# Softplus from the scalar engine's logarithm, the second expert share added there, and cluster prompts summed by steps

## The chip, the cores and the metric

The kernel runs on one core of a Trainium2 chip. A core has five engines, each with its own instruction queue, worked off in order: PE (TensorE, matrix products and transposes into PSUM), DVE (VectorE, element by element), ACT (ScalarE, functions from activation tables, copies, scaling), POOL (GpSimd, which here issues gathers and scatter-adds by row number) and SP (which issues plain DMAs). An engine waits for another only where a semaphore says so. The metric is the device time of one execution in microseconds, the median over several runs.

## The reference

The input `x` is (2, 2048, 256): two batches of 2048 tokens with 256 channels, all in 32-bit floats. Each token is normalised, and three things are added: `x` itself, a state-space scan over the tokens sorted by cluster, and a mixture of experts.

```python
xn = layernorm(x)
# scan branch, per batch
bucket = argmax(l2norm(xn) @ l2norm(means).T)         # 8 clusters
xs     = xn sorted by bucket (stable)
dts, Bm, Cm = split(x_proj @ xs)                      # 32, 16 and 16 rows
Cm    += (means @ prompt_weight.T)[bucket]            # the cluster's prompt
delta  = softplus(dt_proj @ dts + dt_bias)            # 256 channels
h_t    = exp(delta_t * A) * h_(t-1) + delta_t * u_t * B_t   # 16 states a channel
y_t    = sum over states of h_t * C_t + Ds * u_t      # then put back in token order
# expert branch
p1, p2 = softmax of the two largest of xn @ w_gate    # 8 experts
ffn    = sum over the two experts of p * ((silu(xn @ w1) * (xn @ w3)) @ w2)
out    = x + scan + ffn
```

Softplus is log(1 + exp(v)). The kernel writes it as max(v, 0) + log(1 + e) with e = exp(-|v|).

## The kernel before, in words

The front (about the first 65 us) loads `x`, normalises it, finds clusters and experts, and writes the normalised rows with four more columns to the DRAM tensor `xn`. Columns D to D+3 of a row hold the first expert, the second share, the first share minus the second, and the second expert.

From then on two streams of work run interleaved.

*The scan.* The sorted tokens are cut in 8 pieces of 512 (class `Piece`; two batches by four). The 256 channels are two halves `h` of 128 partitions. A piece is prepared by `gather` (four indirect DMAs into `xs`), `turn` (transposes into `u`), `find_members` (which of the 8 clusters each position belongs to, the tile `member`), `project` and `end_projection` (the product `px`, in which `member` by the small matrix `cp` adds the prompts), `load_b` and `load_z` (DMAs that spread rows of B and C) and `step_size`, `square` and `series`, which make `dl` (delta) and `du` (delta by u). Then come 8 steps for each piece (class `Step`: four groups of 4 states by two halves). A step has four places `i`. At each, `feed` makes `bu` on DVE, `scan` runs one recurrence over 512 tokens on DVE, and `decay` makes the `da` of the next step on ACT by an exponential. One step later, `turn` transposes the states on PE into a pair of PSUM buffers (`pt_s`), ACT copies them out (`ht`), and `contract` multiplies them by C on PE into `y`.

*The experts.* The token-expert pairs are sorted into 71 tiles of 128 rows (class `Tile`). A tile has its row gather `load_rows` (tile `xg_sb`, four buffers), `turn` (transposes `pt_g`, the copy `xT`, and the row's share `own`), two `up` products (`p_ps`, with a tanh `t_sb` on ACT, and `silu` and `gate` on DVE), and `down` (product `py`, scaled by `own` on ACT into `yo`, and added to DRAM rows by an indirect DMA on POOL). Weights come by the indirect DMAs `load_up` and `load_down`, three buffers each. A tile that has the same expert as the one three before it is given row numbers out of bounds, so its fetch moves nothing.

*The order.* Every engine's order is the order in which the text emits instructions; a chain of dependencies at the end of the kernel pins it. A planner writes that text. The work on pieces is put at places by `at_place(step, place, ...)`, with place divided by 4 carried into the step. Tile work is a list of `jobs` (two `up` parts and one `down` part for each tile), given out at the places so that the summed PE cost keeps a fixed ratio to the summed DVE cost; the costs are the last two arguments of `at_place`. `silu` and `gate` come two places after their `up`. In the `down` part of tile t the text emits `turn` of tile t+2, the row gather of tile t+5, then the products, `yo` and the scatter-add of tile t, and then the `w_down` fetch of tile t+3; the second `up` part of tile t emits the `w_up` fetch of tile t+3. All these DMAs share POOL's one queue. The first piece is prepared before any step runs, in the list `lead`, one entry after each of the first 13 jobs.

Lines that the prediction's steps touch: the polynomial (L702 `square`, L713 and L718 and L722 `series`), `step_size` (L692 to L698), `own` (L862, L866), `yo` (L902), row gather (L849), weight fetches (L835), scatter-add (L816), gather of a piece (L620), the copies `ht` (L791) and `xT` (L860), the exponential `da` (L760), the scan (L775), the product for the prompts `pc` (L283).

Of the kernel before, what the change touches and what calls it, by code (L numbers as in the profile page):

```python
# [40 lines left out]
F32 = mybir.dt.float32  # L41
BF16 = mybir.dt.bfloat16
I32 = mybir.dt.int32
AF = mybir.ActivationFunctionType
ALU = mybir.AluOpType
# [4 lines left out]
P = 128  # L50
CH = 512
LN_EPS = 1e-5
NORM_EPS_SQ = 1e-24
LOWEST = -3.0e38

LOG1P = (
    (1.0093577, 1.1060627), (-0.08225194, 3.2574694), (-1.424736, 2.702104), (-2.321687, 0.43240654),
)
LOG1P_C = 0.0052326876


@with_exitstack
def scan_moe_kernel(
# [14 lines left out]
    nc = tc.nc  # L78
# [39 lines left out]
    line_of = [cst.tile([P, J], I32, name=f"line_of{b}") for b in range(B)]  # L118
    token_of = cst.tile([P, NT], I32, name="token_of")
    first = [cst.tile([K, NCH], F32, name=f"first{b}") for b in range(B)]  # L120
    last = [cst.tile([K, NCH], F32, name=f"last{b}") for b in range(B)]
    ROWS = B * L + TS
    xn_d = dram.tile([ROWS, D + SH], F32, name="xn")
    acc_d = dram.tile([ROWS, D], F32, name="acc")
# [74 lines left out]
        spare, pattern=[[0, 1]], base=B * L + 1, channel_multiplier=1,  # L199
        allow_small_or_imprecise_dtypes=True,  # L200
    )
    log1p_a = cst.tile([P, len(LOG1P)], F32, name="log1p_a")
    for i, (a, _) in enumerate(LOG1P):
        nc.vector.memset(log1p_a[:, i : i + 1], a)
    zero = cst.tile([P, D + SH], F32, name="zero")
    nc.vector.memset(zero, 0.0)
    te8 = cst.tile([P, NT], F32, name="te8")
# [65 lines left out]
    def small_weights():  # L273

        diag = cst.tile([P, ND, P], F32, name="diag")
        for h in range(ND):
            nc.vector.tensor_scalar(diag[:, h, :], ident, dcol[:, h : h + 1], None, ALU.mult)

        cp = cst.tile([K, XP], F32, name="cp")
        nc.vector.memset(cp, 0.0)  # L280
        pc = ps_m.tile([K, NS], F32, tag="m", name="pc")
        for h in range(ND):
            nc.tensor.matmul(  # L283
                pc, lhsT=chosen_by[:, h, 0:K], rhs=pwT[:, h, :], start=h == 0, stop=h == ND - 1
            )
        nc.vector.tensor_copy(cp[:, R + NS :], pc)

        nc.scalar.activation(na, na, AF.Exp)
        nc.vector.tensor_scalar_mul(na, na, -1.0)
        return diag, cp  # L290
# [146 lines left out]
    def sort_tokens():  # L437
# [55 lines left out]
        nc.vector.tensor_copy(pos, posf)  # L493
        for b in range(B):
            nc.vector.tensor_scalar(first[b], begins, fst[:, b : b + 1], None, ALU.add)
            nc.vector.tensor_scalar(last[b], first[b], cntT[:, b : b + 1], None, ALU.add)
        return pos

    def list_rows(b: int, pos):
# [126 lines left out]
    class Piece:  # L626
# [17 lines left out]
        def find_members(self):  # L644
            b, c = self.b, self.c
            self.member = scn.tile([K, CH], F32, tag="member", name="member", bufs=1)
            nc.vector.tensor_scalar(self.member, at, first[b][:, c : c + 1], None, ALU.is_ge)
            nc.vector.scalar_tensor_tensor(
                self.member, at, last[b][:, c : c + 1], self.member, ALU.is_lt, ALU.mult
            )  # L650

        def project(self, h: int):
            if h == 0:
# [31 lines left out]
        def step_size(self, h: int):  # L685

            if h == 0:
                self.e = pre.tile([P, ND, CH], F32, tag="tok", name="e")
                self.r = pre.tile([P, ND, CH], F32, tag="tok", name="r")
                self.sq = {}  # L690
            pd = ps_m.tile([P, CH], F32, tag="m", name="pd")
            nc.tensor.matmul(  # L692
                pd, lhsT=dtT[:, h * P : (h + 1) * P], rhs=self.xd[0:R, :], start=True, stop=True
            )
            nc.scalar.activation(self.e[:, h, :], pd, AF.Abs, bias=bias[:, h : h + 1])
            nc.scalar.activation(self.r[:, h, :], pd, AF.Relu, bias=bias[:, h : h + 1])  # L696

            nc.scalar.activation(self.e[:, h, :], self.e[:, h, :], AF.Exp, scale=-1.0)  # L698

        def square(self, h: int, i: int):  # L700
            self.sq[h, i] = scn.tile([P, CH], F32, tag="sq", name="sq", bufs=3)
            nc.scalar.activation(  # L702
                self.sq[h, i], self.e[:, h, :], AF.Square, bias=log1p_a[:, i : i + 1]
            )

        def series(self, h: int, i: int):

            if h == 0 and i == 0:
                self.dl = prep.tile([P, ND, CH], F32, tag="dl", name="dl")
                self.du = prep.tile([P, ND, CH], F32, tag="du", name="du")  # L710
            dl = self.dl[:, h, :]
            if i < len(LOG1P):
                nc.vector.scalar_tensor_tensor(  # L713
                    dl, self.sq.pop((h, i)), LOG1P[i][1], dl if i else self.e[:, h, :],
                    ALU.add, ALU.mult,
                )
            elif i == len(LOG1P):
                nc.vector.scalar_tensor_tensor(  # L718
                    dl, dl, LOG1P_C, self.r[:, h, :], ALU.mult, ALU.add
                )  # L720
            else:
                nc.vector.tensor_mul(self.du[:, h, :], dl, self.u[:, h, :])  # L722

        def begin(self, h: int):

# [104 lines left out]
    class Tile:  # L830
# [23 lines left out]
        def turn(self):  # L854
            xg = self.xg
            pt = ps_m.tile([P, ND, P], F32, tag="m", name="pt_g")
            for h in range(ND):
                nc.tensor.transpose(pt[:, h, :], xg[:, h * P : (h + 1) * P], ident)  # L858
            self.xT = ffn.tile([P, ND, TS], F32, tag="xT", name="xT")
            nc.scalar.copy(self.xT, pt)  # L860
            self.own = ffn.tile([P, 1], F32, tag="own", name="own", bufs=6)
            nc.vector.scalar_tensor_tensor(  # L862
                self.own, xg[:, D : D + 1], te8[:, self.t : self.t + 1], xg[:, D + 2 : D + 3],
                ALU.is_equal, ALU.mult,
            )
            nc.vector.tensor_add(self.own, self.own, xg[:, D + 1 : D + 2])  # L866

        def up(self, i: int):
            wk = w13_sb[self.t % NW][:, i * ND * H : (i + 1) * ND * H].rearrange(
# [24 lines left out]
        def down(self):  # L894
            w2 = w2_sb[self.t % NW].rearrange("p (f d) -> p f d", f=NH)
            py = ps_m.tile([P, D], F32, tag="m", name="py")
            for f in range(NH):
                nc.tensor.matmul(  # L898
                    py, lhsT=self.g[:, f, :], rhs=w2[:, f, :], start=f == 0, stop=f == NH - 1
                )  # L900
            yo = ffn.tile([P, D], F32, tag="yo", name="yo", bufs=3)
            nc.scalar.activation(yo, py, AF.Copy, scale=self.own)  # L902
            add_rows(acc_d, [(token_of[:, self.t : self.t + 1], yo)])

# [85 lines left out]
    turn_tile(1)  # L990
    p = pieces[0]

    def first_series(h: int):
        for i in range(len(LOG1P) + 2):
            if i < len(LOG1P):
                p.square(h, i)
            p.series(h, i)


    lead = [  # L1000
        [lambda: list_rows(0, pos)], [p.gather], [], [], [], [lambda: p.turn(0)],
        [lambda: p.turn(1), p.find_members],
        [lambda: p.project(0), lambda: p.project(1), p.end_projection],
        [lambda: p.load_b(0), *(lambda q=q: p.load_z(q) for q in range(NQ)), lambda: p.step_size(0)],
        [lambda: p.step_size(1), lambda: first_series(0)], [lambda: first_series(1)],
        [lambda: p.begin(0), lambda: p.begin(1)], [lambda: p.mask_z(0)],
    ]
    ahead = len(lead)
# [26 lines left out]
    for n, p in enumerate(pieces):  # L1035
        s0 = n * SP_
        for q in range(1, NQ):
            at_place(max(s0 + 2 * q - 3, 0), NSUB - 1 if n or q > 1 else 0, lambda p=p, q=q: p.load_b(q))
        if n:
            s1 = s0 - SP_  # L1040
            at_place(max(s1 - 1, 0), 1 if n > 1 else 0, p.gather)
            for h in range(ND):
                at_place(s1 + 1, 2 + h, lambda p=p, h=h: p.turn(h), 0.5)
                at_place(s1 + 2, 1 + 2 * h, lambda p=p, h=h: p.project(h), 0.95)
                at_place(s1 + 3 + h, 2 - 2 * h, lambda p=p, h=h: p.step_size(h), 1.0)
                for i, place in enumerate(((17, 18, 20, 21, 23, 25), (19, 22, 24, 26, 28, 30))[h]):
                    if i < len(LOG1P):
                        at_place(s1, place - 2, lambda p=p, h=h, i=i: p.square(h, i))
                    at_place(s1, place, lambda p=p, h=h, i=i: p.series(h, i), 0.0, 0.6)
            at_place(s1 + 2, 0, p.find_members, 0.0, 1.2)  # L1050
            at_place(s1 + 3, 0, p.end_projection, 0.95)
            for q, load, use in ((0, 16, 22), (1, 20, 27), (2, 29, 33), (3, 37, 41)):
                at_place(s1, load, lambda p=p, q=q: p.load_z(q))
                at_place(s1, use, lambda p=p, q=q: p.mask_z(q), 0.0, 0.6)
            at_place(s1 + 5, NSUB - 1, lambda p=p: p.load_b(0))
            at_place(s0, 3, lambda p=p: p.begin(0), 0.9)
            at_place(s0 + 1, 1, lambda p=p: p.begin(1), 0.9)
        s2 = s0 + SP_
        to = acc_d if n + 1 < len(pieces) else out_rows
        at_place(s2, 0, lambda p=p: p.take_sums(0))  # L1060
        at_place(s2, 3, lambda p=p: p.take_sums(1))
        at_place(s2 + (n + 1 < len(pieces)), 0 if n + 1 < len(pieces) else 3, lambda p=p, to=to: p.add_sums(to))
# [106 lines left out]
```

## Time and profile before

| what | value |
|---|---|
| three runs | 793.4, 794.46, 795.9 us (median 794.46) |
| profiled execution, its own time | 793.45 us |
| its span, first to last instruction | 791.7 us, 16967 instructions |
| mean granted TensorE clock | 0.951 |
| last expert product `py` starts | 749.1 us |
| last `yt` copy of the scan starts | 779.5 us |
| DMA | 125.90 MB, mean 159 GB/s |

The span is cut in 40 slices of 19.8 us. The first four are the front; the preparation of the first piece lies between 69 and 117 us; the two streams run interleaved from there to about 749 us; after that only the last four scan steps and the output are left. Busy shares are averages over these stages, so a stage is read by its own window. An engine's "idle before" is attributed to the event that released it.

### The profile page before, as it was taken

The numbers are of one execution on the slowest core, as the hardware profiler recorded it, in microseconds if no ns is written. First come the engines' busy times: TensorE is split into PE (matmuls) and PEld (weight loads), VectorE is DVE, ScalarE is ACT, GpSimd is POOL, SyncE is SP. The second block draws the span as 40 slices with busy tenths as digits, with TensorE's granted clock in tenths as the row PEclk, the third lists the DMA queues.
The fourth block names the chain that finished last, engine by engine and source line by source line (L and its number), as shares of the span: only waits on it lengthen the run. The fifth ranks groups of instructions, "written<-read, shape, count | busy, mean of one in ns | idle before, by whom it ended". The sixth has DMA issues, their size and how long they took to land.

```text
span 791.7 us, 16967 instructions
## 1 busy us (share of the span) xinstructions
PE 712.9 (90%) x6552; PEld 605.5 (76%) x6552; DVE 711.3 (90%) x1162; ACT 507.9 (64%) x986; POOL 520.9 (66%) x374
## 2 busy tenths in 40 slices
PE   7385979899999999899999999999999998999963
PEld 5144768589877988599868986798779885998842
DVE  8865269899999999899989999899999998899991
ACT  4821266586669657776668666866687576757572
POOL 2023738657867886788776787878678787686313
PEclk9755999999999999999999999999999998999996
DMA  8593244664368547855656367448644855444462
GB/s 280 222 323 114 58 173 108 210 172 97 108 155 244 154 106 215 203 148 143 206 140 176 56 247 219 107 95 263 197 111 132 273 156 112 107 102 96 86 219 27
DMA packets 61215, 125.90 MB, mean 159 GB/s; under 512 B 24464, under 2 KB 42032, under 8 KB 53776
## 3 DMA queue, kind: packets, MB, share of 16 engines
q0 software_dynamic: 40224, 65.03, 34.6%
q1 hardware_dynamic: 20912, 59.80, 22.1%
q8 instruction: 52, 0.85, 0.4%
q14 instruction: 27, 0.22, 0.1%
HBM read 180.06 MB, written 27.00 MB: 262 GB/s over the span
## 4 chain that ended last, share of the span: by engine, by line
PE 69%; ACT 6%; DVE 3%; issue 3%; DMA 2%; POOL 1%; POOLq 0%; SPq 0%; ACTq 0%; DVEq 0%
PE p_ps L875 28%; PE py L898 14%; PE pt_s L787 12%; PE y L796 6%; ACT ht L791 2%; DMA out_dram<-acc 2%; PE y L728 2%; PE pt_g L858 2%; PE px L655 2%; PE pd L692 1%; DVE hs L775 1%; ACT da L760 1%; DVE bu L766 1%; PE px L660 1%; PE pt_u L641 1%
## 5 line engine op out<-in xcount | busy, mean ns | idle before, releaser
L875 PE MATMUL p_ps<-xT,w 128*128 128x128 f32 x2272 | 280.3, 279 | 5.3 <-ACT sq L702 4.3
L875 PEld LDWEIGHTS p_ps<-xT,w 128*128 128x128 f32 x2272 | 268.2, 195 | 20.2 <-issue 9.3
L775 DVE TENSOR_TENSOR_SCAN hs<-da,carry,bu 128x512 f32<-128x512 f32 x192 | 246.2, 1283 | 0.0
L760 ACT ACTIVATE da<-dl,na 128x512 f32<-128x512 f32 x256 | 182.0, 723 | 1.1 <-DVE hs L775 1.0
L816 POOL DMA_INDIRECT acc<-yo,token_of x71 | 137.8, 1941 | 60.3 <-ACT yo L902 20.0
L766 DVE TENSOR_TENSOR bu<-du,bt 128x512 f32<-128x512 f32 x256 | 174.0, 680 | 0.0
L791 ACT COPY ht<-pt_s 128x512 f32<-128x512 f32 x256 | 137.1, 590 | 31.3 <-PE pt_s L787 31.0
L787 PE MATMUL pt_s<-ident,hs 128*128 128x128 f32 x1024 | 137.9, 279 | 14.7 <-ACT ht L791 8.7
L835 POOL DMA_INDIRECT w<-in_w_up_dram,w_row x71 | 94.8, 1335 | 84.2 <-DVE w_row L584 36.8
L898 PE MATMUL py<-w,g 128*128 128x256 f32 x568 | 139.0, 389 | 12.2 <-ACT r L696 8.7
L787 PEld LDWEIGHTS pt_s<-ident,hs 128*128 128x128 f32 x1024 | 117.7, 143 | 31.6 <-ACT ht L791 15.6
L898 PEld LDWEIGHTS py<-w,g 128*128 128x128 f32 x568 | 104.2, 193 | 27.1 <-ACT r L696 10.3
L849 POOL DMA_INDIRECT xg_sb<-xn,token_of x71 | 88.3, 1243 | 37.5 <-issue 30.2
L835 POOL DMA_INDIRECT w<-in_w_down_dram,w_row x71 | 93.5, 1317 | 21.6 <-issue 12.5
L883 ACT ACTIVATE t_sb<-p_ps 128x512 f32<-128x512 f32 x71 | 42.5, 599 | 69.4 <-PE p_ps L875 69.1
L902 ACT ACTIVATE yo<-py,own 128x256 f32<-128x256 f32 x71 | 33.8, 476 | 80.5 <-PE py L898 80.3
L775 DVE TENSOR_TENSOR_SCAN hs<-da,bu 128x512 f32<-128x512 f32 x64 | 78.2, 1223 | 0.0
L796 PE MATMUL y<-ht,z 128*32 128x128 f32 x2048 | 74.3, 279 | 2.5 <-ACT ht L791 1.9
L816 POOL DMA_INDIRECT acc<-yt,line_of x28 | 54.7, 1952 | 25.7 <-ACT ht L791 8.2
L796 PEld LDWEIGHTS y<-ht,z 128*32 128x32 f32 x2048 | 51.1, 110 | 24.5 <-issue 13.2
L888 DVE SCALAR_TENSOR_TENSOR t_sb<-t_sb,p_ps 128x512 f32<-128x512 f32 x71 | 48.2, 679 | 9.1 <-ACT t_sb L883 8.8
L892 DVE SCALAR_TENSOR_TENSOR g<-t_sb,p_ps 128x512 f32<-128x512 f32 x71 | 48.3, 681 | 7.2 <-PE p_ps L875 4.7
(188 smaller groups left out, 632.8 us busy)
## 6 DMA issues: line engine op xcount, KB each, us to landing
bt<-bc SPq DMA_DIRECT2D x32, 1024.0 KB, 5.4
z<-bc SPq DMA_DIRECT2D x32, 256.0 KB, 3.8
xn<-xt SPq DMA_DIRECT2D x8, 520.0 KB, 2.6
xt<-in_x_dram SPq DMA_DIRECT2D x8, 512.0 KB, 7.5
acc<-in_x_dram SPq DMA_DIRECT2D x8, 512.0 KB, 6.4
w<-in_w_up_dram,w_row POOLq DMA_INDIRECT x71
w<-in_w_down_dram,w_row POOLq DMA_INDIRECT x71
xg_sb<-xn,token_of POOLq DMA_INDIRECT x71
```

Of the source, the lines that this page charges most:

```text
L760: nc.scalar.activation(self.da[i], self.piece.dl[:, self.h, :], AF.Exp, scale=na[:, self.h, n : n + 1])
L766: nc.vector.tensor_mul(self.bu[i], self.piece.du[:, self.h, :], self.piece.bts[self.q][:, i, :])
L775: nc.vector.tensor_tensor_scan(self.hs[:, :, i], self.da[i], self.bu[i], start, ALU.mult, ALU.add)
L787: nc.tensor.transpose(pt[:, j, :], self.hs[:, t0 : t0 + G, :].rearrange("p t n -> p (t n)"), ident)
L791: nc.scalar.copy(self.ht[i], pt)
L796: nc.tensor.matmul(p.ys[self.h][j * G : (j + 1) * G, i, :], lhsT=p.zs[q][:, i * (P // G) + j, :], rhs=self.ht[i][:, j, :], start=False, st ...
L816: ins = nc.gpsimd.indirect_dma_start(out=to, out_offset=bass.IndirectOffsetOnAxis(ap=numbers, axis=0), in_=rows, in_offset=None, compute_o ...
L835: nc.gpsimd.indirect_dma_start(out=to[self.t % NW], out_offset=None, in_=rows, in_offset=bass.IndirectOffsetOnAxis(ap=w_row[:, self.t : se ...
L849: nc.gpsimd.indirect_dma_start(out=self.xg, out_offset=None, in_=xn_d, in_offset=bass.IndirectOffsetOnAxis(ap=token_of[:, self.t : self.t ...
L875: nc.tensor.matmul(p[:, f, :], lhsT=wk[:, h, f * P : (f + 1) * P], rhs=self.xT[:, h, :], start=h == 0, stop=h == ND - 1,)
L892: nc.vector.scalar_tensor_tensor(self.g, self.s, 0.5, self.p3, ALU.mult, ALU.mult)
L898: nc.tensor.matmul(py, lhsT=self.g[:, f, :], rhs=w2[:, f, :], start=f == 0, stop=f == NH - 1)
```

## The change

Three edits are made together.

1. *Softplus.* The polynomial for log(1 + e), e times four quadratics, is replaced; it took four squares on ACT and five multiply-adds on DVE for each half. ACT makes `w` = 1 + e (rounded) and takes its logarithm, one instruction over both halves (128x1024). DVE makes (w - 1) - e, which is what the rounding added, takes it from `r` = max(v, 0), adds `r` to the logarithm and multiplies by `u`, each over both halves at once. The exponential moves out of `step_size` into `decay_of_one`. The planner's places and costs change accordingly.
2. *Share.* `own` is column D+2 where the tile's expert is the row's first one, and zero elsewhere; this is still made on DVE in `Tile.turn`. The addition of the second share moves from there to ACT in `Tile.down`, as the bias of an Identity activation on a 128x1 column, read from `xg`.
3. *Prompts.* `member` is now 1 for every cluster that begins at or before the position, so one comparison makes it. `cp` holds differences between successive clusters' prompts (made from `differ`), so the product sums the steps. The tiles `last` are gone.

```diff
+        differ = cst.tile([P, ND, K], F32, name="differ")
+        nc.vector.tensor_copy(differ[:, :, 0:1], chosen_by[:, :, 0:1])
+        nc.vector.tensor_sub(differ[:, :, 1:], chosen_by[:, :, 1:K], chosen_by[:, :, 0 : K - 1])
...
-                pc, lhsT=chosen_by[:, h, 0:K], rhs=pwT[:, h, :], start=h == 0, stop=h == ND - 1
+                pc, lhsT=differ[:, h, :], rhs=pwT[:, h, :], start=h == 0, stop=h == ND - 1
...
-            nc.vector.tensor_scalar(last[b], first[b], cntT[:, b : b + 1], None, ALU.add)
...
-            nc.vector.scalar_tensor_tensor(
-                self.member, at, last[b][:, c : c + 1], self.member, ALU.is_lt, ALU.mult
-            )
...
+        def decay_of_one(self, h: int):
+            if h == 0:
+                self.w = scn.tile([P, ND, CH], F32, tag="w", name="w", bufs=1)
             nc.scalar.activation(self.e[:, h, :], self.e[:, h, :], AF.Exp, scale=-1.0)
-        def square(self, h: int, i: int):
-            self.sq[h, i] = scn.tile([P, CH], F32, tag="sq", name="sq", bufs=3)
-            nc.scalar.activation(
-                self.sq[h, i], self.e[:, h, :], AF.Square, bias=log1p_a[:, i : i + 1]
-            )
+            nc.scalar.activation(self.w[:, h, :], self.e[:, h, :], AF.Identity, bias=ones[:, 0:1])
+
+        def log(self):
+            self.dl = prep.tile([P, ND, CH], F32, tag="dl", name="dl")
+            nc.scalar.activation(self.dl, self.w, AF.Ln)
+
+        def series(self, i: int):
+            if i == 0:
+                nc.vector.scalar_tensor_tensor(
+                    self.e, self.w, 1.0, self.e, ALU.subtract, ALU.subtract
+                )
+            elif i == 1:
+                nc.vector.tensor_sub(self.r, self.r, self.e)
+            elif i == 2:
+                nc.vector.tensor_add(self.dl, self.dl, self.r)
+            else:
+                self.du = prep.tile([P, ND, CH], F32, tag="du", name="du")
+                nc.vector.tensor_mul(self.du, self.dl, self.u)
...
-            nc.vector.tensor_add(self.own, self.own, xg[:, D + 1 : D + 2])
...
+            nc.scalar.activation(self.own, self.own, AF.Identity, bias=self.xg[:, D + 1 : D + 2])
             nc.scalar.activation(yo, py, AF.Copy, scale=self.own)
...
-        [lambda: p.step_size(1), lambda: first_series(0)], [lambda: first_series(1)],
+        [lambda: p.decay_of_one(0), lambda: p.step_size(1), lambda: p.decay_of_one(1), p.log, lambda: p.series(0),
+         lambda: p.series(1)],
+        [lambda: p.series(2), lambda: p.series(3)],
...
-                for i, place in enumerate(((17, 18, 20, 21, 23, 25), (19, 22, 24, 26, 28, 30))[h]):
-                    if i < len(LOG1P):
-                        at_place(s1, place - 2, lambda p=p, h=h, i=i: p.square(h, i))
-                    at_place(s1, place, lambda p=p, h=h, i=i: p.series(h, i), 0.0, 0.6)
-            at_place(s1 + 2, 0, p.find_members, 0.0, 1.2)
+                at_place(s1, 16 + 2 * h, lambda p=p, h=h: p.decay_of_one(h))
+            at_place(s1, 20, p.log)
+            for i, place in enumerate((21, 22, 25, 26)):
+                at_place(s1, place, lambda p=p, i=i: p.series(i), 0.0, 1.1)
+            at_place(s1 + 2, 0, p.find_members, 0.0, 0.5)
```

In the changed program, as built, ACT's instruction list holds 17 table loads instead of one: one at the start as before, and for each of the 8 pieces one ahead of the logarithm and one ahead of the first exponential or tanh that follows it.

More of the change, by code (lines that the diff above doesn't have):

```diff
@@ L54 @@
 LOWEST = -3.0e38
-LOG1P = (
-    (1.0093577, 1.1060627), (-0.08225194, 3.2574694), (-1.424736, 2.702104), (-2.321687, 0.43240654),
-)
-LOG1P_C = 0.0052326876
 @with_exitstack
@@ L120, in scan_moe_kernel @@
     first = [cst.tile([K, NCH], F32, name=f"first{b}") for b in range(B)]
-    last = [cst.tile([K, NCH], F32, name=f"last{b}") for b in range(B)]
     ROWS = B * L + TS
@@ L201, in scan_moe_kernel @@
     )
-    log1p_a = cst.tile([P, len(LOG1P)], F32, name="log1p_a")
-    for i, (a, _) in enumerate(LOG1P):
-        nc.vector.memset(log1p_a[:, i : i + 1], a)
     zero = cst.tile([P, D + SH], F32, name="zero")
@@ L689, in step_size @@
                 self.r = pre.tile([P, ND, CH], F32, tag="tok", name="r")
-                self.sq = {}
             pd = ps_m.tile([P, CH], F32, tag="m", name="pd")
@@ L696, in step_size @@
             nc.scalar.activation(self.r[:, h, :], pd, AF.Relu, bias=bias[:, h : h + 1])
+        def decay_of_one(self, h: int):
+            if h == 0:
+                self.w = scn.tile([P, ND, CH], F32, tag="w", name="w", bufs=1)
             nc.scalar.activation(self.e[:, h, :], self.e[:, h, :], AF.Exp, scale=-1.0)
-        def square(self, h: int, i: int):
-            self.sq[h, i] = scn.tile([P, CH], F32, tag="sq", name="sq", bufs=3)
-            nc.scalar.activation(
-                self.sq[h, i], self.e[:, h, :], AF.Square, bias=log1p_a[:, i : i + 1]
[L704 to L709, printed above, removed]
-                self.du = prep.tile([P, ND, CH], F32, tag="du", name="du")
-            dl = self.dl[:, h, :]
-            if i < len(LOG1P):
[L713 to L722, printed above, removed]
+            nc.scalar.activation(self.w[:, h, :], self.e[:, h, :], AF.Identity, bias=ones[:, 0:1])
[12 more added lines that the diff above has]
+            else:
+                self.du = prep.tile([P, ND, CH], F32, tag="du", name="du")
+                nc.vector.tensor_mul(self.du, self.dl, self.u)
         def begin(self, h: int):
@@ L991, in scan_moe_kernel @@
     p = pieces[0]
[L993 to L997, printed above, removed]
     lead = [
@@ L1045, in scan_moe_kernel @@
                 at_place(s1 + 3 + h, 2 - 2 * h, lambda p=p, h=h: p.step_size(h), 1.0)
-                for i, place in enumerate(((17, 18, 20, 21, 23, 25), (19, 22, 24, 26, 28, 30))[h]):
-                    if i < len(LOG1P):
-                        at_place(s1, place - 2, lambda p=p, h=h, i=i: p.square(h, i))
-                    at_place(s1, place, lambda p=p, h=h, i=i: p.series(h, i), 0.0, 0.6)
-            at_place(s1 + 2, 0, p.find_members, 0.0, 1.2)
+                at_place(s1, 16 + 2 * h, lambda p=p, h=h: p.decay_of_one(h))
[3 more added lines that the diff above has]
+            at_place(s1 + 2, 0, p.find_members, 0.0, 0.5)
             at_place(s1 + 3, 0, p.end_projection, 0.95)
```

## The prediction

> **What bounds the kernel now.** I read the page first: busy shares, slices, and the chain of work that ended last.
>
> ```profile
> span 791.7 us, 16967 instructions
> ...
> PE 712.9 (90%) x6552; PEld 605.5 (76%) x6552; DVE 711.3 (90%) x1162; ACT 507.9 (64%) x986; POOL 520.9 (66%) x374
> ...
> PE   7385979899999999899999999999999998999963
> ...
> DVE  8865269899999999899989999899999998899991
> ```
>
> PE and DVE look alike, so the shares don't say which one sets the time. Two stretches of the middle, by the table of windows (PE, PEld, DVE, ACT, POOL, clock, DMA share, GB/s):
>
> ```profile
> 180.00:270.00 90.00, 88.42 (x864) 76.80 (x863) 87.59 (x128) 61.90 (x123) 67.83 (x46) 1.00 0.58 157
> 450.00:540.00 90.00, 86.41 (x825) 74.91 (x823) 86.38 (x128) 62.39 (x123) 71.84 (x48) 1.00 0.61 172
> ```
>
> Both are at 96 to 98%. The waits settle it:
>
> ```profile
> PEld pt_s L787 <- ACT ht L791: 15.6, 20, 1.6
> PE py L898 <- ACT r L696: 8.7, 5, 3.1
> PE pt_s L787 <- DVE hs L775: 6.0, 3, 3.3
> ```
>
> PE is released by the scans three times in all, and the timeline puts all three after 762 us, when the expert work is over (1.89 + 3.26 + 0.86 = 6.0 us). In the interleaved stretch PE never waits for a scan; it waits for ACT. The chain of work agrees: 69% of the span on PE, 6% on ACT, 3% on DVE. So PE's own work sets the time, and only PE's gaps can change: from 140 to 750 us they sum to some 18 us, nearly all closed by ACT.
>
> **The change part by part.**
>
> *DVE work.* Out: 96 polynomial instructions (32.2 + 11.0 + 10.7 + 10.7 = 64.6 us in the groups of L713, L718, L722), 71 additions for `own` (11.3), 8 comparisons at L648 (5.9), 2 `last` (0.5). In: 32 instructions of 128x1024. Such a one isn't in the trace; 128x256 takes 0.42 us (L485) and 128x512 0.67, so the estimate is 1.19 us, 38 us in all. Net about 44 us off DVE. What it is worth is a question of cover: PE covers it, as above. I take 0 for the interleaved stretch. Fewer DVE costs also make the planner spread the same `up` and `down` parts more evenly; PE's sum stays.
>
> *ACT work.* Out: 64 squares, 46.4 us. In: 16 Identity at 0.68 (row of L695, also with a pointer bias) = 11; 8 logarithms of 128x1024, 0.63 (Exp, L698) plus 512 elements at the slope between `xT` 0.38 and `ht` 0.59, so 1.05 each = 8.4; 71 additions of `own`, bounded by `carry` (128x4, 0.18) below and 0.3 with a pointer above, 0.25 = 18; and 16 table loads. The trace has one load:
>
> ```profile
> L378 ACT ACT_TABLE_LOAD x1 | 1.3, 1283 | 0.7 <-PEq L1158 0.7
> ```
>
> 16 by 1.28 = 20.5 us. ACT's sum grows by about 12 us, to 66% of the span, and still has room. Where it lands is what counts.
>
> *Around the logarithm.* It stands at place 20 of each piece, behind `carry`, ahead of the `da` and the `ht` copies of the next place. The first such place, in the timeline:
>
> ```profile
> 174.67 0.18 ACT L781 COPY carry<-hs 128x4 f32<-128x4 f32 x1
> ...
> 174.75 0.72 ACT L702 ACTIVATE sq<-e,log1p_a 128x512 f32<-128x512 f32 x1
> ...
> 176.00 1.05 ACT L791 COPY ht<-pt_s 128x512 f32<-128x512 f32 x2
> ...
> 177.97 1.04 PE L787 MATMUL pt_s<-ident,hs 128*128 128x128 f32 x8
> ```
>
> PE makes its third transpose group at 177.97 and needs the first `pt_s` buffer back. With the change ACT runs load 1.28, logarithm 1.05, load 1.28 from 174.75, then `da` 0.61 and `ht` 0.53: the buffer is free at 179.5, so PE stalls 1.5 us. Queued behind the loads are also `xT` and `yo`, which PE needs only two parts later. By the changed order of ACT's queue a part of a tile stands between logarithm and second load in some pieces, or PE has another part ahead of its third transpose, which hides up to 1.8 us. I take 1.3 us for each of the 7 pieces behind the first: +9 us. Here a rule of the Trainium skill speaks against the change: "ScalarE: Activation LUTs", section "What ACT_TABLE_LOAD costs", adds a drain of about 1.38 us to the 1.28 us of the load. Then the pair holds ACT 2.8 us longer, each stall is about 4 us, and the sum is +29 us. The row shows 1.28 but nothing in front of or behind that load to drain, so it can't deny it. I take the row[...]. Both ends stay for the range.
>
> *Places 14 to 19.* There ACT is PE's limit: `py` waited up to 3.13 us for the second `r` (L696), behind `da`, two squares, `carry`. In the new order one Exp and one Identity stand where Exp and two squares stood, 0.6 us less. -0.6 x 7 = -4 us.
>
> *`own` on ACT.* It waits for nothing late, and `yo` waits for it, about 0.3 us. ACT usually sits waiting for `py` there. +1.5 us, for the places where it is behind.
>
> *The buffer that `own` keeps.* Now `xg` is read in `down` of its tile, not in `turn` two tiles earlier. There are four buffers, and the text emits the gather of tile t+4 in the `down` part of tile t-1: its DMA has to wait for `own` of tile t on ACT, one tile later. The built program does show an added ACT wait on each such gather. Behind it on POOL's queue stand the scatter-add, both weight fetches and the piece's gathers. In the lead (timeline):
>
> ```profile
> 73.03 0.96 POOL L849 DMA_INDIRECT xg_sb<-xn,token_of  x1 [0.30 <-issue]
> ...
> 79.78 1.00 POOL L835 DMA_INDIRECT w<-in_w_up_dram,w_row  x1 [5.78 <-PE p_ps L875]
> ...
> 83.33 0.37 ACT L860 COPY xT<-pt_g 128x256 f32<-128x256 f32 x1 [1.41 <-PE pt_g L858]
> ...
> 84.83 0.96 POOL L620 DMA_INDIRECT xs<-xn,line_of  x1 [0.30 <-issue]
> ...
> 87.64 0.33 PE L641 MATMUL pt_u<-ident,xs 128*128 128x128 f32 x1 [0.50 <-DMA xs<-xn,line_of]
> ```
>
> The gather of tile 4 (73.03) can't go before `own` of tile 0, which follows the `xT` copy of 83.33, so at 83.96 instead. Then fetch, and four piece gathers one after another: the last moves from 84.83 to 90.25, 5.4 us later. PE waited for it at 87.64 already, so PE stalls 5.4 us more. Nothing hides this.
>
> Later it hides. Laying POOL's queue out again by its own durations with this one wait added, fetches move by 0 to 9 us. The tightest is at 350.84: it would be issued at 357.6 and is used at 365.52, which leaves 6.5 us behind its issue. The rows of 8 KB of one `w_up` fetch take 3.1 to 6.0 us. A piece's gathers keep at least 1.3 us. I take 0, and up to +10 for the range.
>
> *Front.* `pc` (65.61, PE) now waits for `differ`, behind `diag` on DVE, so to about 68.9 with the transposes `pt_g` queued behind it; the first `up` moves from 69.07 by about +1 us. The two `last` saved are in this.
>
> *Lead.* PE waited 4.34 us at 109.48 for `silu` (108.70 on DVE), which stood behind the whole polynomial of the first half. In the new order only two 1.19 us instructions stand ahead, from 104.2: `silu` at 106.5. -2 us.
>
> Sum: 9 - 4 + 1.5 + 5.4 + 0 + 1 - 2 = +10.9 us on the profiled 793.45, so 804.3. That execution lies 1 us under the median of 794.46, inside the spread of the runs, so I don't add it: **804 us**, its own range 798 to 812.
>
> **The rivals.**
>
> *The drain is paid* (chance 0.15). Load and drain as the skill has it: +29 in place of +9, so about 824; partly absorbed, 815 to 826. For it: the page's measured figure. Against: ACT idles a third of the time and can catch up.
>
> *POOL falls behind* (0.15). POOL is 75 to 80% busy in the middle, some 93% with the 0.30 us between its DMAs. In stretches where tiles follow every 7.2 us the queue already runs without a gap. If the wait costs some fetches their deadline, +1 us on each of the 21 fetches that move data behind the lead, with late piece gathers (5 us): +10, so about 815.
>
> *DVE paces it after all* (0.19), the other side. PE's ends are modelled, so a PE that is held by DVE for tenths of a microsecond would show as busy. Then DVE's 44 us less, some 34 of them in the interleaved stretch, pass on in part; from a third (11 us) on it outweighs the sum. At 60%: 804 - 20 = 784. Against: blocks of 16 `p_ps` products follow one another at 1.79 us over and over, as fast as PE goes anywhere at full clock.
>
> *Nothing to measure* (0.11). The stalls at the logarithm are hidden by tile parts (-9) and the rest balances: 795. It needs PE to hold a part in hand in each piece.
>
> *The forecast* has 0.40.
>
> **How the numbers follow.** Measurement tells 0.3% (2.4 us) from no change. Faster: the DVE case, 0.19. Same: 0.11. Slower: 0.40 + 0.15 + 0.15 = 0.70. The range leaves out half of the DVE case below and the upper half of the drain case above: 787 to 822.
>
> **What would show it.** In the changed profile: 17 table loads of 1.28 us; gaps of 1 to 2 us in `pt_s` <- `ht` beside each of 7 logarithms (4 us if the drain is real); the first piece's `pt_u` waiting some 6 us for `xs`; gathers of rows (L849 before) released by ACT; DVE down to about 667 us with more waits for ACT and PE. If DVE's idle time stays small and the interleaved stretch shrinks, PE was not the limit, and I am wrong in the reading of the waits. If `p_ps` waits for `w` DMAs, the POOL part was wrong.

## The result, and the profile after

The changed kernel takes 815.8 us (median of four runs, 813.0 to 817.3), the kernel before 794.7 us beside it: a ratio of 1.0262, 95% interval 1.0229 to 1.0294. It is slower by 21 us. The forecast was slower by 9.5 us (804, range 787 to 822): the direction holds, the size does not.

The page of the changed kernel, the lines that answer to those shown of before:

```profile
span 813.7 us, 16665 instructions
...
PE 719.2 (88%) x6552; PEld 609.1 (75%) x6552; DVE 673.8 (83%) x1015; ACT 522.5 (64%) x1033; POOL 530.4 (65%) x374
...
PE   7376788999989999999998998999899999999872
...
DVE  8964149789878998989988897889888998899991
```

DVE's busy time has fallen by 37.5 us (711.3 to 673.8); summed over its instructions, overlaps counted twice, it is 44.4 us (786.1 to 741.7), and 44 were forecast. The span has grown by 22. The loss begins early: in the fifth and sixth slices (81 to 122 us) DVE reads 1 and 4 where it read 2 and 6, and PE's fifth reads 7 where it read 9: the first piece comes late. The table of windows (us, then PE, PEld, DVE, ACT, POOL, each with its count of instructions, granted clock, DMA share, GB/s), for the same two stretches as before:

```profile
180.00:270.00 90.00, 85.53 (x809) 74.37 (x808) 77.34 (x102) 62.54 (x128) 65.66 (x45) 0.98 0.55 146
450.00:540.00 90.00, 86.37 (x836) 74.83 (x835) 77.99 (x103) 62.07 (x124) 69.66 (x45) 0.98 0.57 151
```

DVE fell from 97% to 86% of the first stretch, and PE did not rise with the room: it does 809 products there instead of 864, and in both its clock is 0.98 where it was 1.00. The waits say who holds it now (engine, line, what it waited for, us in all, times, longest):

```profile
PE pt_u L635 <- DMA xs<-xn,line_of: 16.6, 9, 3.6
...
PE pt_s L776 <- ACT ht L780: 12.0, 15, 1.6
...
PE p_ps L863 <- ACT xT L849: 5.0, 3, 2.3
```

```profile
POOL xg_sb L838 <- ACT own L890: 77.3, 18, 13.6
```

The first is the largest and new: PE waits 16.6 us for the rows of a piece (`xs`); before it was 0.5 us in all. The second fence is POOL: its row gathers wait 77.3 us for the `own` that the change put on ACT.

Two marks cut the run: the first scan, and the start of the last tile's `py`, the last expert product. The lead, to the first scan, ends at 121.7 us (117.1 before): +4.6. The interleaved stretch from there to the last product takes 648.9 us (632.0): +16.9. The rest is as long as before within a microsecond.

### The profile page after: what moved, and what is told of

It reads as the page before. It is cut to its first block, busy times and chain, and to the rows that moved or that the text cites. A ratio compares the mean times of both kernels' runs of the same rounds, so it can differ in the third digit from the quotient of the medians.

```text
span 813.7 us, 16665 instructions
## 1 busy us (share of the span) xinstructions
PE 719.2 (88%) x6552; PEld 609.1 (75%) x6552; DVE 673.8 (83%) x1015; ACT 522.5 (64%) x1033; POOL 530.4 (65%) x374
## 5 line engine op out<-in xcount | busy, mean ns | idle before, releaser
L863 PE MATMUL p_ps<-xT,w 128*128 128x128 f32 x2272 | 287.7, 283 | 7.6 <-ACT xT L849 5.0
L863 PEld LDWEIGHTS p_ps<-xT,w 128*128 128x128 f32 x2272 | 275.7, 199 | 20.7 <-issue 9.5
L805 POOL DMA_INDIRECT acc<-yo,token_of x71 | 140.6, 1981 | 45.3 <-issue 17.2
L838 POOL DMA_INDIRECT xg_sb<-xn,token_of x71 | 95.5, 1345 | 109.4 <-ACT own L890 77.3
L776 PEld LDWEIGHTS pt_s<-ident,hs 128*128 128x128 f32 x1024 | 114.9, 141 | 38.1 <-ACT ht L780 21.3
L886 PE MATMUL py<-w,g 128*128 128x256 f32 x568 | 137.3, 385 | 6.7 <-ACT u L636 2.0
L805 POOL DMA_INDIRECT acc<-yt,line_of x28 | 52.7, 1881 | 14.2 <-issue 6.4
```

The source lines that it names most:

```text
L776: nc.tensor.transpose(pt[:, j, :], self.hs[:, t0 : t0 + G, :].rearrange("p t n -> p (t n)"), ident)
L805: ins = nc.gpsimd.indirect_dma_start(out=to, out_offset=bass.IndirectOffsetOnAxis(ap=numbers, axis=0), in_=rows, in_offset=None, compute_o ...
L838: nc.gpsimd.indirect_dma_start(out=self.xg, out_offset=None, in_=xn_d, in_offset=bass.IndirectOffsetOnAxis(ap=token_of[:, self.t : self.t ...
L863: nc.tensor.matmul(p[:, f, :], lhsT=wk[:, h, f * P : (f + 1) * P], rhs=self.xT[:, h, :], start=h == 0, stop=h == ND - 1,)
L886: nc.tensor.matmul(py, lhsT=self.g[:, f, :], rhs=w2[:, f, :], start=f == 0, stop=f == NH - 1)
```

## The experiments

Three theories stood against one another.

- *A, the kept buffer.* `xg` is now read by `own` on ACT in `down`, so the gather into that buffer waits, and everything behind it on POOL's one queue is late.
- *B, the tables.* 16 table loads, possibly with a drain each, stop ACT and through it PE.
- *C, the small instructions.* The 71 additions on ACT themselves hold up the work there.

**Six buffers for `xg`.** Takes away what makes the gathers wait; all three edits stay.

```diff
-            self.xg = ffn.tile([P, D + SH], F32, tag="xg", name="xg_sb", bufs=4)
+            self.xg = ffn.tile([P, D + SH], F32, tag="xg", name="xg_sb", bufs=6)
```

> The changed kernel with six buffers for xg instead of four; all else as changed. Theory A (the gather of a later tile waits for the share's addition on ACT because that addition still reads xg; POOL's one queue then issues the pieces' gathers late, and PE stalls in pt_u): the ACT waits of the row gathers go, pt_u waits for xs under 1 us in all instead of 16.6, 799 us (796 to 802). Theory B (the 16 table loads, with drains, hold PE): 813 to 816, as changed. Theory C (the 71 small ACT instructions themselves, with yo waiting behind each, hold PE): 812 to 816.

Measured 791.7 us, ratio to before 0.9935 (0.9907 to 0.9963). One number, and the changed kernel is faster than before: theory A holds, and it is worth 24 to 25 us (815.8 less 791.7, or each counted from the kernel before beside it), more than the whole loss. POOL's largest wait ahead of the row gathers, with six buffers, is no longer one for `own`:

```profile
POOL xg_sb L838 <- issue: 32.2, 54, 16.0
```

The 24 us lie in both parts: the first scan is at 113.7 us instead of 121.7 (8.0), and the stretch is 633.8 us long instead of 648.9 (15.1).

**The share back on DVE.** Takes away the wait and the instructions.

```diff
+            nc.vector.tensor_add(self.own, self.own, xg[:, D + 1 : D + 2])
...
-            nc.scalar.activation(self.own, self.own, AF.Identity, bias=self.xg[:, D + 1 : D + 2])
```

> The changed kernel with the second share's addition put back on DVE, in turn; logarithm and prompts as changed. Theory A: 798 us (795 to 801). Theory B: 812 to 815. Theory C: 797 us. Together with the run with six buffers: if that one is slower by more than 2 us, the small instructions cost that themselves.

Measured 789.16, ratio 0.9913 (0.9888 to 0.9938). Between this and six buffers lie some 2 us (2.5 here, 2.1 by the repeat further down), and the intervals overlap. That is the most that the additions can cost by being on ACT (C).

**The share alone**, on the kernel before: the second edit without the other two.

> The kernel before with the second edit alone (share added on ACT). Theory A: 811 us (807 to 815), with pt_u waiting some 15 us for xs. Theory B: 796 us. Theory C: 811 us.

Measured 825.82, ratio 1.0373 (1.0349 to 1.0397): 30 us slower, twice what theory A had expected, and more than all three edits together. Its PE and POOL waits:

```profile
PE pt_u L641 <- DMA xs<-xn,line_of: 19.3, 13, 3.1
```

```profile
POOL xg_sb L849 <- ACT own L901: 97.4, 26, 11.1
```

**The share alone with six buffers.** The same kernel with the number of the first experiment.

> The kernel before with the second edit alone (share added on the scalar engine), and six row-gather buffers instead of four. The share alone cost 30 us. If all of that but the small instructions is the gather that waits for a late reader of its buffer, 797 to 798 (the before kernel plus some 2.5 for 71 small instructions); if the addition on the scalar engine holds up the work there, it stays above 805.

Measured 795.17 beside 794.69 for before, ratio 1.0013 (0.9993 to 1.0034). The 30 us are gone to the last one. So the whole cost of moving the addition is the buffer it keeps; the 71 instructions cost here 0.5 us, inside what can be measured. Six buffers without the share were not run, but they have nothing to give there: in the kernel before, no row gather behind the first waits longer than 0.3 us for anything. The waits of POOL's row gathers for `own` on ACT are gone, and PE's for `xs` are back to one:

```profile
PE pt_u L641 <- DMA xs<-xn,line_of: 0.5, 1, 0.5
```

**The piece's gathers earlier.** Is it just these four DMAs that are late, or the queue? The changed kernel, with `gather` one step (four places) earlier in the text.

```diff
-            at_place(max(s1 - 1, 0), 1 if n > 1 else 0, p.gather)
+            at_place(max(s1 - 2, 0), 1 if n > 1 else 0, p.gather)
```

> The changed kernel with the pieces' gathers emitted one step (four places) earlier from the third piece on; the row gathers' wait for ACT stays. If it is late piece gathers (xs) that cost the interleaved stretch its 15 us: pt_u waits for xs under 6 us (the lead's and the second piece's), 803 us (800 to 806). If it is late weights or scatter-adds: 812 us or more.

Measured 811.37, ratio 1.019 (1.0161 to 1.0219): 4 us better, where 13 would have been the piece's gathers alone. The waits of PE show the exchange:

```profile
PE pt_u L635 <- DMA xs<-xn,line_of: 8.1, 5, 3.0
PE p_ps L863 <- DMA w<-in_w_up_dram,w_row: 6.2, 4, 2.5
```

The remaining 8.1 us are in the first two pieces, whose gathers already stand at the lead and at the first step; from the third on no piece waits, and a wait for weights stands in its place. So the queue as a whole is late, and which of its DMAs pays is set by their order.

**The softplus alone**, on the kernel before: the first edit without the others.

> The kernel before with the first edit alone (logarithm in place of the polynomial). Theory A: 798 us (794 to 802): stalls of 1 to 2 us at each logarithm, less by what the squares cost. Theory B: 811 to 815. Theory C: 794 to 798.

Measured 798.16, ratio 1.0029 (1.0018 to 1.004). Alone the logarithm does not pay, while together with the prompts (the share on DVE) it gains 5 to 7 us (6.6 above, 5.1 in the repeat). What do the prompts add?

**The prompts alone**, on the kernel before: the third edit.

> The kernel before with the third edit alone (prompts by steps, with the planner's cost of find_members at 0.5 instead of 1.2). If saved DVE time counts for nothing: 794.5 us (793 to 796). If the planner's new order or the DVE time counts as it did on top of the logarithm (9 us there): 785 to 788 us.

Measured 792.34, ratio 0.9961 (0.994 to 0.9981): 2.4 us. Not the 9 that lie between 798.16 and 789.16. But that edit also changes a number by which the planner gives out tile parts, the DVE cost that it books for `find_members`. PE's waits between first scan and last product, the one for `r` before and then those of this kernel:

```profile
PE py L898 <- ACT r L696: 7.7, 4, 3.1
```

```profile
PE pt_u L642 <- DMA xs<-xn,line_of: 3.0, 2, 1.7
...
PE py L896 <- ACT r L694: 1.0, 3, 0.5
```

The wait for `r` has nearly gone although every square still runs on ACT, so it can go without the softplus edit; 3.0 us of waits for `xs`, which were not there before, take part of the gain back.

**The softplus with the planner's number**, and nothing else of the prompts: both comparisons stay.

```diff
-            at_place(s1 + 2, 0, p.find_members, 0.0, 1.2)
+            at_place(s1 + 2, 0, p.find_members, 0.0, 0.5)
```

> The kernel before with the first edit, and with the planner's cost of find_members at 0.5 although it still runs both comparisons: the same instructions as with softplus alone, in another order. If the 9 us between softplus alone and softplus with prompts come from where the planner puts the tiles' parts: 789 to 791 us. If they come from the DVE instructions saved: 797 to 799 us.

Measured 790.24, ratio 0.9925 (0.9903 to 0.9948). The instructions are the same as in the softplus alone, with the tile parts given out by another count, and 7 to 8 us are gone (7.9 by the two medians, 6.9 if each is counted from the kernel before beside it). PE's waits between first scan and last product, first without and then with the new number:

```profile
PE pt_s L778 <- ACT ht L782: 12.8, 13, 2.2
PE py L889 <- ACT r L688: 3.6, 2, 2.7
...
PE p_ps L866 <- ACT xT L851: 1.7, 1, 1.7
```

```profile
PE pt_s L778 <- ACT ht L782: 7.4, 9, 1.6
PE p_ps L866 <- ACT xT L851: 4.9, 3, 2.3
```

These waits for ACT fall from 18.1 to 12.3 us; the one for `r` is gone. Why just this order is better was not traced further.

**No table loads.** The share on DVE as above, and the logarithm left out: an Identity of the same size stands in its place, so `dl` is not log(1 + e), and one table load is left of 17.

```diff
-            nc.scalar.activation(self.dl, self.w, AF.Ln)
+            nc.scalar.activation(self.dl, self.w, AF.Identity)
```

> The kernel with the share on DVE, and Identity in place of the logarithm over the same 128x1024; the logarithm itself is left out, so that none of the 16 table loads is needed (delta is then not softplus). If the loads stall PE by the gaps that its trace shows beside the logarithms (some 9 us in all): 780 us (778 to 783). If the loads are hidden: 788 us. If each load also paid a drain[...], the loads' trace rows would show a gap behind them, and this run would be 15 us or more faster.

Measured 781.72, ratio 0.9823 (0.9801 to 0.9846), so the 16 loads cost some 7 us: 7.4 by the two medians, 6.4 if each is counted from the kernel before beside it. PE's waits in the stretch, first with loads (share on DVE) and then without:

```profile
PE pt_s L776 <- ACT ht L780: 7.4, 9, 1.6
PE p_ps L864 <- ACT xT L849: 4.9, 3, 2.3
```

```profile
PE pt_s L776 <- ACT ht L780: 5.1, 6, 1.0
```

2.3 us of the waits for `ht` go, and 4.6 of the 4.9 for `xT`. PE's idle time in the stretch falls by less, 4.8 us in all (18.9 to 14.0), since a wait of 1.4 us for a `w_down` DMA and some shorter ones stand there now; 1.7 us come from its clock (the last section). The stretch is 7.7 us shorter (630.7 to 623.0). In the timeline of the changed kernel such a place, ACT and then PE:

```profile
182.65 0.18 ACT L770 COPY carry<-hs 128x4 f32<-128x4 f32 x1
182.84 1.28 ACT L697 ACT_TABLE_LOAD   x1
184.13 1.06 ACT L697 ACTIVATE dl<-w 128x1024 f32<-128x1024 f32 x1
185.20 1.28 ACT L749 ACT_TABLE_LOAD   x1
186.49 0.72 ACT L749 ACTIVATE da<-dl,na 128x512 f32<-128x512 f32 x1
187.12 1.05 ACT L780 COPY ht<-pt_s 128x512 f32<-128x512 f32 x2
```

```profile
187.74 1.14 PE L776 MATMUL pt_s<-ident,hs 128*128 128x128 f32 x8 [1.63 <-ACT ht L780]
```

The load starts when `carry` ends (182.83) and the logarithm when the load ends: nothing is drained that takes time. PE stalls 1.63 us for `ht`.

**The logarithm three places later**, with the share on DVE: `log` stands behind the `ht` copies of its step instead of in front of them.

```diff
-            at_place(s1, 20, p.log)
+            at_place(s1, 23, p.log)
```

> The changed kernel with the second share's addition back on the vector engine, and the logarithm put at place 23 instead of 20, behind the first transposed copies of its step. Table loads cost about 7 us in the version with the logarithm at place 20. If that price is the transposed copies that stand behind the loads, most of it goes: 784 to 786. If it is spread over everything that follows on the scalar engine, the time stays at 789; if the vector engine then runs late with delta, over 791.

> The changed kernel with the second share's addition back on the vector engine, once more beside the version with the later logarithm, to compare the two on one chip: 789.

Measured 784.42 (ratio 0.9882, 0.9858 to 0.9906) for the later place, beside 789.6 (0.9932, 0.991 to 0.9955) for the version with place 20. 5 us come back, most of what the loads cost. PE's waits in the stretch, with place 23:

```profile
PE pt_s L776 <- ACT ht L780: 5.1, 6, 1.0
PE p_ps L864 <- ACT xT L849: 2.0, 4, 1.2
```

This version (first and third edit, addition on DVE, logarithm at place 23) is the fastest that computes the whole: 10 us under the kernel before.

## Why the prediction was right or wrong

The sum of the prediction, term by term, with what the runs show for each:

| step | forecast, us | measured, us | from |
|---|---|---|---|
| loads around the logarithm | +9 | +7.4 | share on DVE, with and without loads |
| places 14 to 19 | -4 | -4.1, and -7.7 with the planner's order | waits of `py` for `r`: 8.7 before, 4.6 with the softplus alone, 1.0 in the changed kernel |
| `own` on ACT | +1.5 | +0.5 to +2.5 | alone, and in the changed kernel, buffer effect taken out |
| `own` keeps the buffer, lead | +5.4 | +8.0 | first scan, four against six buffers |
| `own` keeps the buffer, later | 0 | +15.1 | stretch, four against six buffers |
| front | +1 | +0.4 | first `p_ps`, 69.07 to 69.48 |
| lead, first piece on DVE | -2 | -3.8 | first scan before to six buffers (-3.4), less the front |

**The step that failed** is the one that said of the kept buffer "Later it hides", with its "A piece's gathers keep at least 1.3 us. I take 0". It had the right mechanism and the right queue, but put this term at nothing. It measured 15.1 us, of which 11.4 are waits of PE for `xs`. The delay of 0 to 9 us that it reckoned for the fetches holds for the gathers too: those of pieces 1 to 6 lose 4.9 to 8.7 us of their cover against before (the table below). As far as its text tells, it set their issue against the time of use; counted so, little is left, as it said. The rows come later than that: in the changed kernel the `xs` gathers of pieces 1 to 6 take 2.7 to 6.0 us from issue to landing, median 4.8 (the 10 of 24 for which the records have a landing). Here is what the kept buffer left of the cover, from the end of the last gather's issue to PE's first transpose of `xs`, in the eight pieces (from the three timelines):

| piece | 0 | 1 | 2 | 3 | 4 | 5 | 6 | 7 |
|---|---|---|---|---|---|---|---|---|
| before, us | 0.9 | 7.4 | 10.3 | 5.4 | 11.5 | 8.7 | 9.1 | 4.7 |
| after with six buffers, us | 1.6 | 5.3 | 10.1 | 5.4 | 8.5 | 12.0 | 8.7 | 7.4 |
| after, us | -1.8 | 0.0 | 2.9 | 0.5 | 4.3 | 0.9 | 0.4 | 7.4 |

Before and with six buffers, every piece behind the lead had some 4.7 us or more, and none made PE wait. Now five of them do (1, 2, 3, 5, 6), all with less than 3 us left. Piece 1 in the timeline of the changed kernel, on POOL and then on PE:

```profile
134.77 2.14 POOL L614 DMA_INDIRECT xs<-xn,line_of  x1 [0.30 <-issue]
```

```profile
136.91 0.49 PE L635 MATMUL pt_u<-ident,xs 128*128 128x128 f32 x3
140.99 0.33 PE L635 MATMUL pt_u<-ident,xs 128*128 128x128 f32 x1 [3.59 <-DMA xs<-xn,line_of]
```

Three of four row blocks are there; PE goes on with the fourth 6.2 us after its issue. Such stalls are 11.4 us in the stretch. Of its 15.1 us over six buffers, PE's idle time makes 11.6 (21.7 to 33.3) and its clock 3.4 (the last section).

**The lead** was the best-argued part, and the shape came as written. The row gather that went at 73.03 waits 13.57 us, and the piece's gathers follow one after another (timeline of the changed kernel, POOL, then PE):

```profile
85.54 0.96 POOL L838 DMA_INDIRECT xg_sb<-xn,token_of  x1 [13.57 <-ACT own L890]
...
91.87 0.95 POOL L614 DMA_INDIRECT xs<-xn,line_of  x1 [0.30 <-issue]
```

```profile
90.97 0.30 PE L635 MATMUL pt_u<-ident,xs 128*128 128x128 f32 x1 [2.79 <-DMA xs<-xn,line_of]
...
94.97 3.38 PE L863 MATMUL p_ps<-xT,w 128*128 128x128 f32 x15
```

PE stalls four times, 5.3 us in all where it was 0.5, and 5.4 more were forecast (83.96 for the row gather, which came at 85.54). Then 15 products take 3.38 us at half clock; at full clock 16 take 1.79 to 1.95. With six buffers PE does not stall there, and 1.7 us less go to the clock between 84 us and the first scan. Stalls and clock are 7.0 of the 8.0 us; the clock was not in the forecast.

**The loads** were right by the row of 1.28 us, and the drain of the Trainium skill ("ScalarE: Activation LUTs", section "What ACT_TABLE_LOAD costs": 1.38 us on top of the load) was not there: a load starts at most 0.02 us after the instruction before it, and the logarithm 0.01 us after its load. With the drain the term was +29. The measured 7.4 is not 7 stalls of 1.3: with the share on DVE the largest three behind the first piece, of 1.63, 2.29 and 1.74 us, are 5.7 us together, and at the other four pieces no stall above 0.9 us stands beside a load. It also said that `xT` behind the loads is needed only two parts later; yet two of these three are PE waiting for `xT`.

**The gains** were taken too small. Without the buffer's effect the prediction's sum is +5.5; six buffers give -4.1 against the kernel before beside it (795.79). So the direction came out right through the buffer alone, and the rest had the wrong sign. The forecast of -4 for the squares met what the softplus alone shows, where the wait for `r` falls by 4.1 us; since that edit changes planner costs too, this does not show that the squares did it. What was missing is the planner's own order, which the prediction took as neutral ("PE's sum stays"): it takes the rest of the wait for `r`, and is worth 7 to 8 us on top of the softplus and 2.4 with the prompts alone.

**PE as the bound** stands. With six buffers DVE has 38 us less to do than before (711.3 to 673.2), and the stretch is as long as before (633.8 against 632.0). The share alone with six buffers is the cleaner case: DVE's busy time falls by 10 us (711.3 to 700.9), and the time stays (795.17 beside 794.69). The rival in which DVE paces the kernel would have shown here. Of the rivals the one that came true is *POOL falls behind*, at 815 and with a chance of 0.15, and its number is luck: the terms it names, 21 fetches at 1 us and 5 us for the gathers, add up to 26 us and not to 10. Measured, it is the gathers, 11.4 us behind the lead; the one wait for weights there is 1.9 us, and with six buffers it is 1.8.

## What to carry to other kernels

When a reader of a buffer moves to a later point, ask first which producer refills that buffer, and what else stands behind that producer in its queue; a tiny instruction moved from DVE to ACT cost 30 us here because it kept one of four buffers for longer, and two more buffers gave it all back. Cover is to be counted from a transfer's landing to its use, not from its issue. Where a new instruction holds an engine for 3.6 us, its place in the queue counts: three places later, behind the copies that PE waits for, gave back 5 of the 7 us that its loads cost. And a planner that works by booked costs is part of the change: one such number was worth 7 to 8 us with the same instructions.

## What the runs showed of the hardware

Stalls of PE can cost more than their length, through its clock. In the stretch of the changed kernel the granted clock falls to 0.50 four times, each time for 3.41 us. This starts at 156.22, 234.73, 490.73 and 579.48 us; the distances are 23, 75 and 26 times 3.413 us, in the records to a hundredth of a step. So the steps lie on a fixed grid, and the table of windows can be cut by it (columns as above):

```profile
231.29:234.70 3.41, 1.23 (x11) 0.93 (x9) 3.41 (x5) 1.78 (x4) 2.90 (x2) 1.00 0.64 239
234.70:238.12 3.42, 3.32 (x16) 3.32 (x17) 0.12 (x2) 1.21 (x2) 2.02 (x2) 0.50 0.66 77
...
135.72:139.13 3.41, 1.68 (x14) 1.34 (x12) 3.41 (x6) 2.05 (x4) 2.80 (x3) 1.00 0.91 319
139.13:142.55 3.42, 1.56 (x14) 1.56 (x15) 2.25 (x4) 0.59 (x1) 2.81 (x3) 1.00 0.54 111
142.55:145.96 3.41, 3.41 (x55) 3.09 (x54) 2.18 (x3) 2.42 (x5) 2.80 (x3) 1.00 0.19 43
...
152.80:156.22 3.42, 2.00 (x19) 1.24 (x17) 1.06 (x3) 0.68 (x2) 2.83 (x2) 1.00 0.95 322
156.22:159.63 3.41, 3.41 (x19) 3.41 (x18) 3.15 (x7) 0.00 (x0) 0.99 (x1) 0.50 0.55 137
439.53:442.94 3.41, 1.51 (x7) 0.97 (x6) 3.41 (x6) 3.38 (x5) 2.80 (x3) 1.00 0.47 90
442.94:446.35 3.41, 2.97 (x26) 2.97 (x27) 3.41 (x6) 1.94 (x6) 2.74 (x3) 1.00 0.91 351
```

A stall of 2.28 us that falls into one step leaves PE busy for 1.23 of 3.41 us, and the next step runs at half clock: 16 products in it, and half of its 3.41 us, about 1.7, lost. The longest stall of the stretch, 3.59 us, is cut by the grid into two steps that are busy for 1.68 and 1.56 us, and costs no clock. PE's busy time in the step ahead does not settle it, though. Ahead of the other three low steps it was 2.00, 1.58 and 1.47 us, while a step with 1.51 us (439.53 to 442.94) was followed by full clock. What else decides, these records do not tell; PE's ends in them are modelled. The Trainium skill ("TensorE: Matmul & The Clock Gate", section "HAM oscillation — how this bites in real kernels") warns of idle gaps above some 3.4 us; here low steps followed stalls of 1.42, 2.28, 1.83 and 2.06 us, and none followed the longest two in the stretch, of 3.59 and 2.35 us. In the kernel with the share alone and four buffers, 15.4 us of its stretch are lost this way, with six buffers 5.1. So of the 27.3 us by which that stretch is longer with four buffers, 15.5 are PE's idle time and 10.2 its clock.

Left open: PE's time in the stretch that is neither idle nor lost to the clock is 608.7 us in the changed kernel with six buffers and 608.8 with four, before 605.5. A few products more fall into the stretch (17 and 3), and no wait in the records accounts for these 3 us.
